# Every second normalization of the last block on VectorE, unread products moved ahead of the deviation, and two block orders replaced, in a four-part residual kernel on one Trainium2 core

## The chip, the cores and the metric

The kernel runs on one core of one Trainium2 chip. The metric is the device time of one execution in microseconds (us). It was taken in three timed runs; one more execution was profiled. The engines are TensorE (PE; its weight loads are shown as PEld), VectorE (DVE), ScalarE (ACT), GpSimd (POOL) and SyncE (SP), which issues most of the transfers. Each engine takes its own instructions in the order in which they were recorded, and they wait for each other by semaphores.

## The reference

x is 128 sequences of 64 tokens with 256 features, in float32. Four parts are added to it in turn, each conditioned on one vector per sequence:

```python
x = x + L0(x, cond)   # kx = modulated_linear(x); softmax attention over 16 heads of one token; modulated_linear
x = x + L1(x, cond)   # up(relu(down(x))) + x, with weights scaled by sequence
x = x + L2(x, ...)    # below
x = x + L3(x, cond)   # a matrix per sequence of rank 30, and a bias
```

The change lies in L2, which normalizes each token three times:

```python
def _ln(x, g, b):
    m = jnp.mean(x, axis=-1, keepdims=True)
    v = jnp.mean((x - m) ** 2, axis=-1, keepdims=True)
    return (x - m) * jax.lax.rsqrt(v + EPS) * g + b
h = _ln(x, pw_g[pathway_ids], pw_b[pathway_ids])      # gains gathered by token
h = _ln(h, cp_g[compartment_ids], cp_b[compartment_ids])
t = _ln(x, tm_g[time_steps], tm_b[time_steps])        # s is alike, with ms_g, ms_b
cat = concatenate([w[0]*h, w[1]*t, w[2]*m, w[3]*n, w[4]*r, w[5]*s])
return _ln(silu(cat @ int_W1 + b1) @ int_W2 + b2, int_g, int_be)
```

Here t and s share the deviation of x, so there are three sets of statistics: of x, of the gathered state h, and of the second layer's output y.

## The kernel before, in words

The 8192 tokens are worked on in 16 blocks (0 to 15) of 512 tokens (8 sequences), each of 4 tiles of 128 tokens. A prologue makes what doesn't depend on the tokens. For each block `attention` does L0 and `rest` does L1, L2 and L3. Block n + 1's attention is worked on beside block n's rest; after block 15's attention nothing is left to run beside its rest but what remains of block 14.

The program first lists all operations with their reads and writes, and a planner (`Plan`) then puts them in an order. Within an engine it picks among the operations that can start first the one of the lowest priority number. The numbers come from tables written into the kernel (`TURNS`): one for the prologue, one each for the first, second, last but one (14) and last (15) block, and one for the middle blocks; a block's number times 400 is added. The planner also hands out buffers, among them four PSUM banks for everything but the attention scores. What the planner emits is the order of each engine's queue.

The steps of `rest` that matter, with the lines of the profile before:

- The two up-products of L1 (L1223) give, with VectorE (L1236), the state x2T, which is features by tokens. TensorE transposes it (L1273), ScalarE copies the four tiles out (L1276), and VectorE makes the statistics (L469, L470).
- `rstd` and `offset` run on GpSimd: add epsilon (L474), the mean negated (L1253), the power -1/2 (L476), and the product of the two (L1254). They leave r and nr for x, rh and nrh for h, and ry and nry for y.
- `normalize` (L1259) is an ACTIVATE of ScalarE with scale r and bias nr, one for each tile.
- GpSimd multiplies and adds the gathered gains (L1284, L1290), whose gathers it issues itself (L940). h is normalized, xn and h are transposed (L1308), ScalarE copies them out (L1311), gains are products with a one-hot matrix (L1317) that VectorE multiplies in (L1326).
- The first layer's products (L1344 with weights w_x, w_t, w_s, w_h, and L1353 for biases), tanh (ScalarE, L1359) and VectorE (L1362) give s2. The second layer's products (L1387, one pair for each tile), an eviction with a bias (VectorE, L1392) and statistics follow.
- y is normalized (L1259 again) and scaled by GpSimd (L1403), which also adds x2 (L1406). TensorE transposes (L1418). In the last block alone the transposes take the normalized tiles themselves, VectorE evicts them with gain and state (L1424), and GpSimd's two steps run beside that. L3's two products (L1445, L1471) with VectorE between (L1456) follow, VectorE adds the tile (L1479), and SP writes it out (L1483).

In the last block (`quick`) six groups of unread products stand between the second layer and L1418. A group (`keep`) is one small product that reads its gate, and so waits for it (L444), and then n products of the identity with itself (L446) into a bank that nobody reads. Gates and n before: mvy, ry and nry with 4 each, and the first three normalized tiles with 3 each.

The wider attention steps that the order moves are the scores (L1071), their maxima (VectorE, L1080), the shift (L1121), the exponentials (ScalarE, L1135), the products with the values (L1146), their transpose and reciprocal (VectorE, L1158, L1162), the scaling (GpSimd, L1165), a transpose (L1176) and the output projection (L982).

Of the kernel before, what the change touches and what calls it, by code (L numbers as in the profile page):

```python
# [13 lines left out]
ALU = mybir.AluOpType  # L14
# [8 lines left out]
NTILE = T // 128  # L23
# [35 lines left out]
class Plan:  # L59
# [163 lines left out]
    -10633 41137 464 10909 -44878 -11608 -42604 -45090 10155 -44468 -500 -500 -500 -500 -500 -500  # L223
# [53 lines left out]
    -945 -5006 28741 3292 -555 -2679 4333 19756 13246 29426 3507 42507 949 -1489 14772 22434 -2092 33522 31798 41815  # L277
    951 30003 36734 39833 31441 44287 36835 36712 48388 -2211 33995 35152 6414 18014 27987 -10794 26523 6071 13167
    215 -9627 40936 -4357 6419 10572 4571 -7266 41550 17576 2454 32076 31767 -2728 16615 41208 837 4340 8765 36154
    -10880 4665 -558 -2062 4662 -3798 1273 31044 36706 35521 -1668 -419 19391 3818 26245 31507 24910 28317 -6286  # L280
    26998 -11618 25996 12900 26677 40415 20947 4197 4591 -10897 34316 29621 46596 6494 -4361 -5325 30488 28382 33266
    18048 33066 30258 -4468 44044 39446 3045 11442 54 3568 3791 -5774 -2389 836 17585 32107 3610 3509 11677 27998
    5918 -289 -3076 10611 22471 8317 24462 31609 27367 -11407 5640 5006 25531 6317 12721 12013 -6353 39363 7446 4072
    -1182 -2303 33420 5842 -3197 -3385 30659 31515 868 756 5023 33464 5290 34805 27086 29256 -2628 -4019 6625 33507
    3780 1799 30520 32280 29029 46575 20997 32367 9369 29333 -3611 1761 5073 23038 -2673 4124 -3837 18828 -210 5311
    32964 13572 -5042 815 27152 -6571 45385 6618 32189 18218 25530 13431 4354 28866 27343 42996 27711 28905 48852
    20499 25821 12505 19373 -5371 3342 27949 30404 6752 33874 -4408 26737 -9042 5014 33335 43087 44864 12794 42849
    4268 28770 21167 7601 9132 29149 5277 5277 5277 29004 31538 -2220 3845 8107 955 30135 3881 -4854 -7113 4074 30336
    11443 -2251 -580 -6078 4549 -2314 4266 11515 36765 1109 1500 5145 34519 17201 5779 33709 -5975 31030 14097 11178
    37473 23054 11112 -11491 27939 12681 11926 21735 35542 -1369 28928 27461 806 30077 -4774 23069  # L290
    """,
    "last": """
    -918 -4932 28785 3332 -569 37576 95 19583 13303 29612 3564 42657 5172 -1432 14778 22470 -2127 33487 31798 41753
    970 30025 36750 39866 31463 44309 36857 36734 48399 29838 33987 35461 6445 18036 28009 -10772 26548 6113 13077
    237 -9611 40952 -4341 6378 10566 11434 -7289 41527 17553 -2664 32185 32004 -2665 16815 41408 1037 4540 8965 36354
    -10831 4624 -604 -2085 4601 -3493 1256 17026 36681 35506 -1449 -434 19376 3801 25885 18811 24911 28352 -6303
    26981 -11699 25941 12883 26660 40398 20930 37525 4574 -10945 34299 29411 46591 6473 3726 -5383 30451 28410 33294
    18120 33105 30216 -4508 44002 39404 2964 11361 -166 3348 3579 -5994 -2333 610 18563 31899 3363 3325 4560 27779
    5744 -463 -3063 10622 -5376 8328 24473 31758 33518 -11396 5316 4677 43337 5936 12777 11684 -6037 39679 7352 3989
    -1170 -2067 33534 5696 -3081 -3304 30916 3513 1082 969 -1348 33586 5412 34403 27208 29378 -11701 -4005 6612 27354  # L300
    3767 1811 -9041 32275 33374 46570 20992 32362 9366 29381 -3588 1701 5121 4398 17015 4312 -3658 31671 -173 5447
    33077 13685 12794 -1508 27373 -6586 45375 6606 32445 18219 25520 13404 4325 28839 16940 42969 36247 29019 48820
    20465 25794 12337 -1583 -5541 3161 27768 30224 6612 33693 -4589 26551 -9304 4752 33073 42825 44576 12454 42500
    3902 28515 20894 7574 8848 28753 4872 4872 4993 28720 31263 -2335 3579 7833 -1601 29984 3730 -5005 -7186 4016
    30266 11356 -2321 -666 -6056 7806 -2377 11778 11029 36263 589 994 4678 34088 16701 5288 33069 -6488 30973 13881
    11108 37403 22984 11042 -11060 27869 3313 11805 21661 19322 -1441 28856 27558 772 29993 -4858 10564
# [5 lines left out]
def resid_chain(ctx: ExitStack, tc: tile.TileContext, a: dict, out: bass.AP, nblk: int = NBLK):  # L312
# [8 lines left out]
    nc = tc.nc  # L321
# [869 lines left out]
    def rest(blk, x1T, pw, oh, wdn, wup, tab, uT):  # L1191
# [64 lines left out]
        def normalize(dst, src, r, nr, tl):  # L1256
            act(
                256,
                lambda: nc.scalar.activation(  # L1259
                    dst.t, src.t, AF.Identity, bias=nr.t[:, tl : tl + 1], scale=r.t[:, tl : tl + 1]  # L1260
                ),
                [src, r, nr],
                [dst],
                more=0.186,
            )
# [130 lines left out]
        if quick:  # L1396
            for value in (mvy, ry, nry):
                keep(4, (value, lambda value=value: value.t.rearrange("p n k -> p (n k)")[:, :4] if value is mvy else value.t))
        for tl in range(NTILE):
            normalize(yn[tl], x3[tl], ry, nry, tl)  # L1400
            if quick and tl < NTILE - 1:
                keep(3, (yn[tl], lambda tl=tl: yn[tl].t[:, :4]))
# [206 lines left out]
```

## Time and profile before

| | us |
|---|---|
| timed runs | 897.63, 900.80, 904.46 |
| median | 900.8 |
| profiled execution | 894.98 |
| its span | 893.2 |

Shares of the span: TensorE 93%, VectorE 71%, GpSimd 68%, weight loads 60%, ScalarE 50%. In the slices of the page the granted clock of TensorE is full between the prologue and the last slices. The chain that ended last is TensorE's for 54% of the span, GpSimd's for 18%, VectorE's for 13%, ScalarE's for 6% and transfers' for 3%.

How to read the lines of the timeline: start and busy time in us, engine, line of the kernel, operation, output and input by the program's names, shapes, and how many; in brackets the time for which the engine stood idle before, and what ended it. A wait for several semaphores is put down to the one that came last. The profiled execution is a single one; its row durations are used as they are.

### The profile page before, as it was taken

The page shows a single profiled execution, that of the slowest core. Times are in us where ns is not written, and L with a number is a line of the kernel's source. Part 1 is how long each engine was busy: PE and PEld are TensorE (multiplying, and loading weights), DVE is VectorE, ACT ScalarE, POOL GpSimd, SP SyncE. Part 2 cuts the span into 40 slices and gives each one's busy share as a digit, 9 for nine tenths or more (in the row PEclk, how much of TensorE's full clock was granted, in tenths as well). Part 3 has the DMA queues.
Part 4 walks back from the last instruction along what each step waited for, and adds up shares of the span by engine and source line. Part 5 has one row for each costly group of instructions (what it writes and reads, how often), then busy time and mean ns, then how long its engine had stood idle before and what let it go on. Part 6 is the DMA issues. An engine that isn't in the chain of part 4 may idle for free.

```text
span 893.2 us, 24076 instructions
## 1 busy us (share of the span) xinstructions
PE 830.2 (93%) x9806; PEld 539.8 (60%) x9806; DVE 638.4 (71%) x1365; ACT 446.9 (50%) x825; POOL 608.0 (68%) x826
## 2 busy tenths in 40 slices
PE   4669999999999999999999999999999999999886
PEld 3548746656665756666566657566666667565435
DVE  3779867868685878777785858777776858586533
ACT  1454444545564555545555645555555556453330
POOL 5563673949687695959596886959595968845333
PEclk9889999999999999999999999999999999999998
DMA  8768742233423242332334232423324332102000
GB/s 252 210 160 251 243 127 64 67 85 103 123 84 116 73 119 82 95 94 73 117 88 125 85 111 69 128 77 92 101 74 117 84 97 84 48 11 64 1 24 25
DMA packets 62575, 90.24 MB, mean 101 GB/s; under 512 B 6328, under 2 KB 46200, under 8 KB 62464
## 3 DMA queue, kind: packets, MB, share of 16 engines
q1 hardware_dynamic: 57344, 71.92, 28.1%
q0 software_dynamic: 5120, 16.78, 6.0%
q8 instruction: 77, 1.26, 0.6%
q14 instruction: 34, 0.28, 0.1%
HBM read 75.44 MB, written 13.24 MB: 99 GB/s over the span
## 4 chain that ended last, share of the span: by engine, by line
PE 54%; POOL 18%; DVE 13%; ACT 6%; issue 5%; DMA 3%; SPq 0%; DVEq 0%; ACTq 0%; POOLq 0%
PE bank L1344 19%; PE sc L1071 4%; PE bank L982 4%; PE bank L1387 4%; PE bank L1015 4%; PE bank L1146 4%; DVE mt L1080 3%; POOL wdn L956 2%; PE sc L1121 2%; POOL kxe L1029 2%; PE bank L1058 2%; PE bank L1176 2%; POOL uu L1290 2%; PE bank L1317 1%; POOL xsT L925 1%
## 5 line engine op out<-in xcount | busy, mean ns | idle before, releaser
L1135 ACT ACTIVATE e<-sc 128x1024 f32<-128x1024 f32 x128 | 125.9, 1023 | 78.3 <-PE sc L1121 78.3
L1080 DVE TENSOR_REDUCE mt<-sc 128x8 f32<-128x1024 f32 x128 | 151.9, 1205 | 16.2 <-PE sc L1071 13.6
L1165 POOL TENSOR_TENSOR att<-ao,rz 128x256 f32<-128x256 f32 x45 | 28.1, 625 | 76.2 <-DVE rz L1162 75.9
L1326 DVE TENSOR_TENSOR uu<-uu,bank 128x512 f32<-128x512 f32 x96 | 63.9, 681 | 16.4 <-PE bank L1317 15.8
L1015 PE MATMUL bank<-wk,xsT 128*128 128x256 f32 x256 | 71.0, 413 | 0.9 <-POOL xsT L925 0.8
L1344 PE MATMUL bank<-uu,w_s 128*128 128x512 f32 x128 | 66.7, 604 | 0.8 <-DVE uu L1326 0.8
L1344 PE MATMUL bank<-uu,w_t 128*128 128x512 f32 x128 | 65.0, 618 | 0.5 <-DVE uu L1326 0.5
L1344 PE MATMUL bank<-x2T,w_x 128*128 128x512 f32 x128 | 64.7, 607 | 0.0
L1387 PE MATMUL bank<-w,uu 128*128 128x256 f32 x256 | 61.8, 385 | 1.9 <-DVE uu L1362 1.9
L1015 PEld LDWEIGHTS bank<-wk,xsT 128*128 128x128 f32 x256 | 48.8, 202 | 19.1 <-issue 11.1
L982 PE MATMUL bank<-osT,wo 128*128 128x512 f32 x128 | 59.2, 604 | 0.5 <-DVE osT L1181 0.5
L1344 PE MATMUL bank<-uu,w_h 128*128 128x512 f32 x128 | 58.7, 595 | 0.5 <-DVE uu L1326 0.4
L474 POOL TENSOR_SCALAR ry<-mvy 128x4 f32<-128x4 f32 (+1 forms) x19 | 4.4, 232 | 77.7 <-DVE mvy L470 77.6
L1090 ACT COPY mt<-mt 128x16 f32<-128x16 f32 x64 | 13.1, 204 | 84.4 <-DVE mt L1080 84.4
L469 DVE BATCH_NORM_STATS2 st<-uu 128x6 f32<-128x256 f32 x119 | 48.5, 418 | 8.1 <-ACT uu L1276 5.0
L1029 POOL TENSOR_TENSOR kxe<-kxe,kbr 128x256 f32<-128x256 f32 x64 | 46.8, 732 | 9.0 <-DVE kxe L1023 6.6
L1387 PEld LDWEIGHTS bank<-w,uu 128*128 128x128 f32 x256 | 45.9, 190 | 9.4 <-DVE uu L1362 3.1
L1023 DVE TENSOR_TENSOR kxe<-bank,dmk 128x256 f32<-128x256 f32 x64 | 26.8, 419 | 30.3 <-PE bank L1015 25.6
L956 POOL TENSOR_TENSOR wdn<-gdb,late 128x512 f32<-128x512 f32 x32 | 40.6, 1272 | 11.4 <-PE bank L1205 6.0
L940 POOL DMA_INDIRECT pw<-in_pw,idx x39 | 40.0, 1024 | 8.0 <-issue 7.4
L970 POOL TENSOR_TENSOR wup<-wup,ubb 128x512 f32<-128x512 f32 x32 | 40.6, 1269 | 3.7 <-DMA ubb<-ugub 1.5
L1103 ACT ACTIVATE mX<-bank,early 128x128 bf16<-128x128 f32 x64 | 23.6, 369 | 38.3 <-PE bank L1096 38.3
(217 smaller groups left out, 2135.9 us busy)
## 6 DMA issues: line engine op xcount, KB each, us to landing
xT<-in_xT SPq DMA_DIRECT2D x32, 256.0 KB
gdb<-dgdb SPq DMA_DIRECT2D x16, 512.0 KB
ubb<-ugub SPq DMA_DIRECT2D x32, 256.0 KB
wup<-ugub SPq DMA_DIRECT2D x32, 256.0 KB
dmk<-demod_k SPq DMA_DIRECT2D x30, 256.0 KB
out_x<-uu SPq DMA_DIRECT2D x35, 128.0 KB
ud<-uu SPq DMA_DIRECT2D x8, 512.0 KB
uT<-ud SPq DMA_DIRECT2D x16, 256.0 KB
```

The costliest lines, as they stand in the source:

```text
L469: dve(256, lambda: nc.vector.bn_stats(st.t, x.t), [x], [st])
L940: lambda tl=tl, n=n: nc.gpsimd.indirect_dma_start(out=pw[tl].t, out_offset=None, in_=a["pw"], in_offset=bass.IndirectOffsetOnAxis(ap=idx[: ...
L956: lambda w=w, dp=dp: nc.gpsimd.tensor_tensor(w(), gdb.t[:, :, 0:64], dp, ALU.mult),
L970: pool(1.25, lambda w=w: nc.gpsimd.tensor_tensor(w(wup), w(wup), w(ubb), ALU.add), [wup, ubb], [wup])
L982: nc.tensor.matmul(ps.t, owT[:, c, bass.ts(oc, 128)], osT.t[:, c, :], start=(c == 0), stop=(c == C - 1))
L1015: nc.tensor.matmul(ps.t[:, :F], xsT.t[:, c, bass.ts(tl, 128)], kwT[:, c, :], start=(c == 0), stop=(c == C - 1))
L1029: lambda: nc.gpsimd.tensor_tensor(kxe.t[:, :, 0:D], kxe.t[:, :, 0:D], heads(kinds["kbr"][0]), ALU.add),
L1080: lambda two=two: nc.vector.tensor_reduce(mt.t[:, two, 0:4], sc.t[:, two, :].rearrange("p q (g n) -> p q g n", g=4), AX.X, ALU.max),
L1135: lambda k=k: nc.scalar.activation(es[k].t, sc.t[:, 2 * k : 2 * k + 2, :], AF.Exp, scale=0.25),
L1326: lambda ps=ps, src=src, dst=dst, c=c: nc.vector.tensor_tensor(dst.t[:, c, :], src.t[:, c, :], ps.t, ALU.mult),
L1344: lambda ps=ps, w=w, src=src, fc=fc, c=c, n=n: nc.tensor.matmul(ps.t, w.t[:, c, bass.ts(fc, 128)], src.t[:, c, :], start=(n == 0 and c == ...
L1387: nc.tensor.matmul(ps.t[:, :F], s2.t[:, c, bass.ts(tl, 128)], w2.t[:, c, :], start=(c == 0), stop=(c == C - 1))
```

## The change

`normalize` takes every second tile (1 and 3) of the last block to VectorE, as a TENSOR_SCALAR with two columns (multiply, add), for all three normalizations of the block. Six instructions leave ScalarE's queue and stand in VectorE's. The groups of unread products get new gates and sizes: the four evicted tiles of the second layer with 3 each, mvy with 2, ry with 2; nry and the normalized tiles are no longer gates. That is 6 gates and 16 unread products in place of 6 and 21. Their six priorities go from -500 to 9000. Both tables of 14 and 15 are replaced as a whole.

```diff
--- before.py
+++ after.py
     "prologue": """
...
-    -10633 41137 464 10909 -44878 -11608 -42604 -45090 10155 -44468 -500 -500 -500 -500 -500 -500
+    -10633 41137 464 10909 -44878 -11608 -42604 -45090 10155 -44468 9000 9000 9000 9000 9000 9000
...
     "last but one": """
-    -945 -5006 28741 3292 -555 -2679 4333 19756 13246 29426 3507 42507 949 -1489 14772 22434 -2092 33522 31798 41815
...
+    25677 -9159 -4970 30441 -3888 33267 7456 2098 33469 22707 27320 30575 2712 35226 25625 29202 4770 2224 6807 48124
...
     "last": """
-    -918 -4932 28785 3332 -569 37576 95 19583 13303 29612 3564 42657 5172 -1432 14778 22470 -2127 33487 31798 41753
...
+    1830 -11952 33325 34973 32324 30258 13163 7005 30022 29679 4280 13204 14222 32365 21347 34327 15721 34598 36025
...
         def normalize(dst, src, r, nr, tl):
+            if quick and tl % 2:
+                dve(
+                    256,
+                    lambda: nc.vector.tensor_scalar(
+                        dst.t, src.t, r.t[:, tl : tl + 1], nr.t[:, tl : tl + 1], ALU.mult, ALU.add
+                    ),
+                    [src, r, nr],
+                    [dst],
+                    0.05,
+                    pair=True,
+                )
+                return
             act(
                 256,
...
         if quick:
-            for value in (mvy, ry, nry):
-                keep(4, (value, lambda value=value: value.t.rearrange("p n k -> p (n k)")[:, :4] if value is mvy else value.t))
+            for tl in range(NTILE):
+                keep(3, (x3[tl], lambda tl=tl: x3[tl].t[:, :4]))
+            keep(2, (mvy, lambda: mvy.t.rearrange("p n k -> p (n k)")[:, :4]))
+            keep(2, (ry, lambda: ry.t))
         for tl in range(NTILE):
             normalize(yn[tl], x3[tl], ry, nry, tl)
-            if quick and tl < NTILE - 1:
-                keep(3, (yn[tl], lambda tl=tl: yn[tl].t[:, :4]))
```

Lines from L1257 on stand 12 lower in the changed kernel (L1418 is L1430, L1479 is L1491, and so on), and L1260 is VectorE's normalization.

What the new tables do to the queues, as the two built programs show it:

- All queues are the same up to TensorE's up-products of block 13 (L1223); what follows differs on every engine. TensorE's and ScalarE's products and copies are the same ones, in another order.
- Block 13 to 14: the shift L1121 stands behind the transposes L1273 instead of ahead of them; on VectorE the transpose L1158 stands between the two maxima; on ScalarE two key copies stand ahead of the third normalization; on GpSimd the scaling L1165 stands behind five h operations instead of three.
- Block 15's attention: its last scores and value products stand two to four first-layer products earlier; between the last value products and the last attention transpose stand two short products (L1353), and all four second-layer products of block 14 follow the transpose.
- Block 15's rest: six of the eight transposes L1273 stand ahead of block 14's L1418; ScalarE's two copies of block 14's state stand ahead of the fourth tile's copy; half of block 14's last products (L1471) stand between the products with w_t.
- The end: the first group of unread products stands between the second and the third second-layer product, the other groups behind the fourth, and the transposes L1418 behind the group of ry. VectorE's last four additions start with tile 0, which is the last that GpSimd finishes.

## The prediction

> **What bounds the kernel now.** I read the page first (its busy shares, then the clock), then the chain of waits of the last 30 us, then the timeline of each engine there, then windows of one clock period. The page says that the kernel is limited by TensorE nearly everywhere:
>
> ```profile
> PE 830.2 (93%) x9806; PEld 539.8 (60%) x9806; DVE 638.4 (71%) x1365; ACT 446.9 (50%) x825; POOL 608.0 (68%) x826
> ```
>
> The two engine orders part for the first time at PE's up-products at 746.14 us, so only the last 147 us of the 893.2 can move. Until 834 PE there is nearly always busy; behind it the last block runs alone. Its end, as TensorE, GpSimd, ScalarE and VectorE did it (start, duration, line, count, and in brackets the idle time before):
>
> ```profile
> 871.34 3.72 PE L1387 MATMUL bank<-w,uu 128*128 128x256 f32 x16 [1.41 <-DVE uu L1362]
> 877.88 0.39 PE L444 MATMUL bank<-ry,ident 128*128 128x4 f32 x2 [1.70 <-POOL ry L476]
> 878.12 1.69 PE L446 MATMUL bank<-ident 128*128 128x128 f32 x8
> 879.60 0.43 PE L444 MATMUL bank<-nry,ident 128*128 128x4 f32 x2
> 879.89 2.05 PE L446 MATMUL bank<-ident 128*128 128x128 f32 x8
> ...
> 883.77 0.91 PE L446 MATMUL bank<-ident 128*128 128x128 f32 x6
> 884.52 0.27 PE L1418 MATMUL bank<-ident,uu 128*128 128x128 f32 x1
> ```
>
> ```profile
> 877.90 0.20 POOL L1254 TENSOR_TENSOR nry<-nry,ry 128x4 f32<-128x4 f32 x1
> 878.82 0.73 POOL L1403 TENSOR_TENSOR p<-uu,late 128x256 f32<-128x256 f32 x1 [0.71 <-ACT uu L1259]
> ...
> 883.72 0.72 POOL L1406 TENSOR_TENSOR uu<-uu,p 128x256 f32<-128x256 f32 x1
> ```
>
> ```profile
> 878.14 0.60 ACT L1259 ACTIVATE uu<-p,nry,ry 128x256 f32<-128x256 f32 x1 [7.58 <-POOL nry L1254]
> ...
> 879.63 0.58 ACT L1259 ACTIVATE uu<-p,nry,ry 128x256 f32<-128x256 f32 x1
> ```
>
> ```profile
> 888.40 1.16 DVE L1479 TENSOR_TENSOR p<-bank,p 128x256 f32<-128x256 f32 x3 [0.87 <-PE bank L1471]
> 889.48 0.42 DVE L1479 TENSOR_TENSOR uu<-bank,uu 128x256 f32<-128x256 f32 x1
> ```
>
> The reader is to see that the four normalizations are done at 880.21, but that the transposes, which need nothing else, start at 884.52: TensorE takes its queue in order, and the unread products stand in it until then. They are work on the path, not cover. The windows give the cause of half of it:
>
> ```profile
> 851.20:854.60 3.40, 2.12 (x13) 1.20 (x12) 2.81 (x8) 2.43 (x5) 3.40 (x6) 1.00 0.43 143
> 854.60:858.00 3.40, 3.40 (x5) 1.15 (x6) 1.35 (x5) 0.00 (x0) 2.47 (x6) 0.51 0.00 0
> 868.20:871.60 3.40, 1.99 (x6) 0.74 (x5) 1.38 (x2) 1.20 (x2) 0.00 (x0) 1.00 0.00 0
> 875.10:878.50 3.40, 1.70 (x14) 1.51 (x14) 1.06 (x5) 0.36 (x1) 1.66 (x4) 1.00 0.00 0
> 878.50:881.90 3.40, 3.40 (x19) 3.40 (x18) 0.00 (x0) 1.71 (x4) 3.08 (x5) 0.51 0.02 5
> ```
>
> Each row is a stretch: length, then busy time of PE, PEld, DVE, ACT, POOL, then the granted clock. Two thin stretches (1.70 and 2.12 us of PE in 3.4) are followed by one at clock 0.51; one with 1.99 is not (871.60 to 875 ran at 1.00), so the share alone doesn't decide.
>
> **The tail, from nry to the end.** Let R be the end of nry (878.10). Before: 893.20 - 878.10 = 15.10 us. In the new orders TensorE meets after R only the eight transposes; two normalizations are ScalarE's and two VectorE's.
> - TensorE's path: 0.04, two ScalarE normalizations (878.14 to 879.23, 1.09), 0.04, and from the transposes on the old 893.20 - 884.52 = 8.68: R + 9.85.
> - GpSimd's path: the eight multiplications and additions (878.82 to 884.44, 5.62) were hidden under unread products and now are not. They start behind VectorE's first normalization. No row of the last block shows it; the nearest is the prologue's 128x256 TENSOR_SCALAR by two columns (L747, mean 404 ns), against 590 of ScalarE. Then VectorE's four additions (888.40 to 889.90, 1.50; the first in the new order needs GpSimd's last result) and 3.30 to the end: R + 0.04 + 0.40 + 0.08 + 5.62 + 0.08 + 1.50 + 3.30 = R + 11.02.
> - VectorE's second normalization runs as GpSimd wants to start. In the prologue the same cast (L508, 128 wide rows, f32 to bf16) took 0.29 us at 47.57 and 1.15 at 43.48, beside a GpSimd operation that ended at 44.5; so one may hold the other. Bounds: 0 and the whole 0.40 (less the 0.08 that GpSimd waits anyway). I take 0.32: R + 11.34.
>
> So GpSimd takes TensorE's place as the last: 15.10 - 11.34 = **3.76 us less**. [...]
>
> **Unread products ahead of R.** The first x3 group of the new order stands between the second and the third second-layer product. One group of three with its gate took 0.12 + 0.77 = 0.89 in the chain (882.90 to 883.79, full clock). VectorE needs 0.86 a tile (872.50, 873.37, 874.23), as long as TensorE, so nothing hides it: **0.89 more**. The other groups run while statistics, ry and nry are made: from 875.96, three of 0.89 and two of 0.12 + 0.51 end at 879.9, and the transposes are wanted at R' + 1.17 = 880.16. That cover is thin: at clock 0.5 the groups would end at 883.9, TensorE's path would be 3.7 longer than R + 9.85, and would pass GpSimd's by 2.2.
>
> **Statistics of x and of the gathered state.** There VectorE takes two normalizations as well (1.09 instead of 2.07). Ahead of them the new order has ScalarE write both halves of block 15's transposed state (0.68 and 0.60) before the fourth tile's copy, which costs about 0.75 of that; and the first transposes (851.96) waited not for ScalarE but for a bank that VectorE's additions of 851.39 freed, which stays. Taken at nothing, between -0.7 and +0.7. VectorE's normalizations there stand before those additions, two to each wait for nr, at 0.8 us in a stretch where VectorE was idle (847.3 to 849.75). GpSimd's three gathers of the last block keep their place behind the h multiplications; SP's loads only swap neighbours, and no wait in this stretch ends on a DMA: nothing, or 1 us if a gather came late.
>
> **The orders.** TensorE's work is the same, so waits are counted, taking each engine's queue in its new order with the old rows:
> - Last but one block, 746 to 770: old waits 0.84 and 0.16. In the new order two key copies stand in ScalarE ahead of the third normalization, so the transposes of xn wait 0.5, the attention transposes 0.75 for GpSimd (its multiplication now stands behind five h operations instead of three) and a gain product 0.3; the sc shift moved behind the x2 transposes saves some. Net +0.65, bounds 0 and +1.4.
> - Last attention tiles, 808 to 835: old waits 0.49 + 0.83 + 0.52 = 1.84. New: after the last e-products only two short products cover the chain transpose, reciprocal, multiplication (832.43 to 834.20), so 1.25, but then four products cover the rest: about 1.4 in all. Net -0.4, bounds -1.2 and 0.
> - Last block, 854 to 870: the 0.78 wait before w_s (861.03) goes, since other products stand there, among them 0.35 of block 14's output. Net -0.43, bounds -2.2 (the half-clock stretch, 3.4 us for 1.7 of work, not entered) and +1.
>
> Sum: -3.76 + 0.89 + 0 + 0.65 - 0.40 - 0.43 = **-3.05 us**. The profiled execution took 894.98 (span 893.20); 891.93 is 0.9966 of it, and of the median 900.8 this is **897.7**. The profiled one lies below all three timed (897.63 to 904.46), so the ratio is used.
>
> [...]
>
> **Rivals.**
> - The orders close more than I can trace (0.30). The waits listed in PE's timeline from 800 to 871.34 add up to 8.9, and the half-clock stretch is 1.7. Two thirds of the first (5.9), the second, and the tail's 2.9 are 10.5: 890.2. For it: the waits come from short chains, which another order can cover. Against: the largest (1.31 for x1T, 1.41 for s2) stand in both orders behind the same instructions.
> - The cover fails (0.13): the clock halves in the unread products. The tail gains 0.66 instead of 2.87: about 900. For it: it halved at 878.50 in this trace. Against: the groups now leave no pause behind the products.
> - The new waits throttle TensorE through the last block (0.07), the side on which it is slower. Place: 844.5 to 870, where products of block 14 no longer fill the wait for x2T (843.2 to 844.5) and a wait of 0.7 for ScalarE's half appears. From 844.5 to 870 PE is busy for 23.3 us, 3.4 of them at half already; if three quarters of the other 19.9 ran at half they would cost 15, less the 3: 912. It decides from the point where most 3.4 us stretches are as thin as the two that were followed by a fall (1.70 and 2.12 us); the new waits alone do not make them so.
> - The change doesn't act: excluded for the normalizations (six instructions stand on VectorE instead of ScalarE), possible for the searched orders, which is in my range.
>
> **How the numbers follow.** The forecast has 0.50, its own range 893 to 901.5. Range over all: 888.5 to 902; it takes in the rival at 890.2 and leaves out the throttled one and outer tails. One per cent is 9 us, about what the three timed runs (6.8 apart) can tell. Faster by over 1%: the first rival, 0.30; slower: the throttled one with an outer tail, 0.08; within: 0.62.
>
> **What would show it.** Tail: transposes about 1.2 after nry, and VectorE's first L1491 waiting on GpSimd, not TensorE. Nry 0.9 later after the first second-layer product than 6.8 us. An unread group between second and third product. GpSimd's first multiplication 0.4 late. Wrong if the transposes still start behind unread products, if the last additions follow TensorE, or if the clock's low stretches multiply after 840.

## The result and the profile after

No measurable change. Fourteen runs of the changed kernel had a median of 901.89 us, fourteen of the kernel before beside them 903.02: ratio 0.9988, 95% interval 0.9968 to 1.0008. Run again later, beside runs of before with a median of 893.49, it was 1.0009 (0.9992 to 1.0027). The forecast was 0.9966.

The page of the changed kernel's profile begins:

```profile
span 900.1 us, 24059 instructions
...
PE 833.0 (93%) x9796; PEld 537.1 (60%) x9796; DVE 639.4 (71%) x1371; ACT 444.6 (49%) x819; POOL 608.0 (68%) x826
```

Its span is 6.9 us longer than before's, but it was 8.42 us behind where the programs part (754.56 against 746.14), so the spans can't be compared. The last stretch can: from the first up-product of block 13 to the end. Each kernel was profiled a second time (before_again, after_again, below). All stages are in us; "s2" is the end of VectorE's last L1374 (L1362 in before), "nry" the end of GpSimd's nry, called R in the prediction, and the stage from nry to the end of the span is the tail. Ends are taken from the span as the page rounds it, so the tail is good to 0.05.

| stage | before | before_again | after | after_again |
|---|---|---|---|---|
| block 13 to 14 (first up-products) | 49.22 | 49.21 | 52.02 | 51.03 |
| block 14 to 15 | 46.64 | 46.63 | 45.66 | 45.66 |
| block 15 to s2 | 29.28 | 27.60 | 28.28 | 28.28 |
| s2 to the end of nry | 6.82 | 6.81 | 7.28 | 7.29 |
| nry to the end of the span | 15.10 | 15.24 | 12.30 | 12.26 |
| last stretch | 147.06 | 145.49 | 145.54 | 144.52 |

The tail did become what the change set out to make of it. TensorE's timeline in the changed kernel (start, busy time; in brackets the wait before):

```profile
879.50 0.70 PE L1399 MATMUL bank<-w,uu 128*128 128x256 f32 x2 [0.33 <-DVE uu L1374]
880.57 1.56 PE L1399 MATMUL bank<-w,uu 128*128 128x256 f32 x6 [0.38 <-DVE uu L1374]
...
882.11 0.92 PE L446 MATMUL bank<-ident 128*128 128x128 f32 x6
882.86 1.89 PE L1399 MATMUL bank<-w,uu 128*128 128x256 f32 x8
...
888.08 0.69 PE L446 MATMUL bank<-ident 128*128 128x128 f32 x4
888.61 0.27 PE L1430 MATMUL bank<-ident,uu 128*128 128x128 f32 x1
```

GpSimd's and VectorE's timelines there:

```profile
887.60 0.20 POOL L1254 TENSOR_TENSOR nry<-nry,ry 128x4 f32<-128x4 f32 x1
888.40 0.77 POOL L1415 TENSOR_TENSOR p<-p,late 128x256 f32<-128x256 f32 x1 [0.60 <-DVE p L1260]
...
893.24 0.72 POOL L1418 TENSOR_TENSOR p<-p,p 128x256 f32<-128x256 f32 x1
```

```profile
887.84 0.42 DVE L1260 TENSOR_SCALAR p<-p,ry,nry 128x256 f32<-128x256 f32 x1 [1.94 <-POOL nry L1254]
888.17 0.41 DVE L1260 TENSOR_SCALAR uu<-uu,ry,nry 128x256 f32<-128x256 f32 x1
...
893.99 0.76 DVE L1491 TENSOR_TENSOR p<-bank,p 128x256 f32<-128x256 f32 x2 [2.16 <-POOL p L1418]
894.66 0.75 DVE L1491 TENSOR_TENSOR uu<-bank,uu 128x256 f32<-128x256 f32 x2
```

The transposes start 0.81 behind nry instead of 6.42, and VectorE's first addition waits 2.16 us for GpSimd. The last addition ends at R + 7.61, earlier than the forecast's R + 8.04. But from it to the end of the span are 4.69 us, where before has 3.30. The chain of waits of the profile ends at that addition and says nothing of this. The closing instructions of the queues do; before and after (queue, count, shortest/median/longest duration in ns, first and last start in us):

```profile
...
L1605 POOLq DRAIN  x3: 45/102/6078, 883.7 to 892.9; - x3
L1605 SPq DRAIN  x3: 7/7/7, 892.4 to 892.7; - x3
```

```profile
...
L1617 POOLq DRAIN  x3: 45/102/6635, 892.6 to 899.8; - x3
L1617 SPq DRAIN  x3: 7/7/7, 898.0 to 899.5; - x3
```

In both, GpSimd's queue ends with a DRAIN of more than 6 us (6.08 and 6.64). In before it lasted from 883.7 to 889.8, under TensorE's tail; SyncE, whose listed waits there have 0.8 us for the output transfers, came to its first drain at 892.4, later than the other engines to theirs, and to its last at 892.7. In the changed kernel it lasts from 892.6 to 899.2; SyncE is at its first drain at 898.0 and at its last only at 899.5. In both the DRAIN ends 5.3 us after GpSimd's last instruction (884.44 and 893.96).

### The profile page after: what moved, and what is told of

The parts are those of the page before. It is cut to its first block, busy times and chain, and to the rows that moved or that the text cites. A ratio compares the mean times of both kernels' runs of the same rounds, so it can differ in the third digit from the quotient of the medians.

```text
span 900.1 us, 24059 instructions
## 1 busy us (share of the span) xinstructions
PE 833.0 (93%) x9796; PEld 537.1 (60%) x9796; DVE 639.4 (71%) x1371; ACT 444.6 (49%) x819; POOL 608.0 (68%) x826
## 3 DMA queue, kind: packets, MB, share of 16 engines
q8 instruction: 77, 1.26, 0.6%
## 4 chain that ended last, share of the span: by engine, by line
PE 74%; DVE 10%; ACT 6%; issue 4%; POOL 3%; DMA 2%; SPq 0%; POOLq 0%; DVEq 0%; ACTq 0%
PE bank L1356 21%; PE sc L1071 8%; PE bank L1399 6%; PE bank L982 6%; PE bank L1146 6%; PE bank L1015 6%; DVE mt L1080 4%; PE bank L1058 2%; PE sc L1121 2%; PE bank L1176 2%; ACT uu L1323 2%; PE bank L1223 2%; PE bank L1329 2%; PE bank L1205 2%; PE bank L1430 1%
## 5 line engine op out<-in xcount | busy, mean ns | idle before, releaser
L1165 POOL TENSOR_TENSOR att<-ao,rz 128x256 f32<-128x256 f32 x45 | 28.0, 623 | 78.9 <-DVE rz L1162 70.0
L1338 DVE TENSOR_TENSOR uu<-uu,bank 128x512 f32<-128x512 f32 x96 | 63.6, 679 | 16.9 <-PE bank L1329 16.4
L1158 DVE STREAM_TRANSPOSE ao<-bank 128x512 f32<-128x512 f32 x45 | 32.0, 712 | 19.0 <-PE bank L1146 19.0
```

Of the source, the lines that this page charges most:

```text
L1338: lambda ps=ps, src=src, dst=dst, c=c: nc.vector.tensor_tensor(dst.t[:, c, :], src.t[:, c, :], ps.t, ALU.mult),
```

## The experiments

All twelve were made from the two kernels. The tables of orders can be exchanged, and the groups of unread products can be moved by their priority. Ratios are to before, in runs on the same chip.

**1. code_alone.** The new code with before's two order tables; the priority of the unread groups is raised so that all stand behind the fourth second-layer product.

```diff
-    -10633 41137 464 10909 -44878 -11608 -42604 -45090 10155 -44468 9000 9000 9000 9000 9000 9000
+    -10633 41137 464 10909 -44878 -11608 -42604 -45090 10155 -44468 60000 60000 60000 60000 60000 60000
...
     "last but one": """
-    25677 -9159 -4970 30441 -3888 33267 7456 2098 33469 22707 27320 30575 2712 35226 25625 29202 4770 2224 6807 48124
+    -945 -5006 28741 3292 -555 -2679 4333 19756 13246 29426 3507 42507 949 -1489 14772 22434 -2092 33522 31798 41815
...
     "last": """
-    1830 -11952 33325 34973 32324 30258 13163 7005 30022 29679 4280 13204 14222 32365 21347 34327 15721 34598 36025
+    -918 -4932 28785 3332 -569 37576 95 19583 13303 29612 3564 42657 5172 -1432 14778 22470 -2127 33487 31798 41753
...
```

> Both block orders are those of before; VectorE's normalizations and the new unread groups are in, and all six groups stand behind the fourth second-layer product. The 'last stretch' is measured from the first up-product of block 13 to the end of the span (before 147.06 us, after 145.54). Theory A (the tail gains what it gained in after, 2.80, and the order of the last-but-one block is what ate it): blocks 13 to 14 (first up-product to first up-product) take 49.3 as before, nry stays 6.8 behind the first second-layer product, the tail from nry to the end is 12.3, the half-clock stretch near the first products of block 15 is still there; last stretch 144.3, ratio to before 0.997. Rival B (the 4.69 us from the last addition to the end, against 3.30, were only that one execution's): tail 10.9, last stretch 142.9, ratio 0.995. Rival C (with before's orders the unread products run at half clock and TensorE ends last): tail 13.5 or more, ratio 0.999.

Ratio 1.0042 (1.0029 to 1.0056): slower, which none of the theories had. The tail is 12.29 as in A, and blocks 13 to 15 are before's, but block 15 to s2 takes 34.69 us. TensorE's waits from 841.5 to 876.3 (us in total, times, longest), the first three:

```profile
PE bank L1356 <- DVE uu L1338: 2.1, 2, 1.2
PE bank L1399 <- DVE uu L1374: 1.8, 1, 1.8
PE bank L1320 <- DVE uu L1260: 1.3, 1, 1.3
```

and VectorE's timeline where the third of them is made:

```profile
850.94 0.76 DVE L1491 TENSOR_TENSOR uu<-bank,uu 128x256 f32<-128x256 f32 x2 [0.96 <-PE bank L1483]
851.61 0.43 DVE L469 BATCH_NORM_STATS2 st<-p 128x6 f32<-128x256 f32 x1
...
852.86 0.38 DVE L1260 TENSOR_SCALAR uu<-uu,r,nr 128x256 f32<-128x256 f32 x1
```

The second of x's normalizations given to VectorE stands there behind block 14's last additions and two statistics of h, 4 us after nr was ready. The thin work is followed by stretches at half clock:

```profile
862.70:866.10 3.40, 1.99 (x5) 0.68 (x5) 1.88 (x3) 0.63 (x2) 0.00 (x0) 1.00 0.00 0
866.10:869.50 3.40, 3.40 (x5) 1.34 (x4) 0.00 (x0) 0.00 (x0) 0.00 (x0) 0.51 0.00 0
```

(length, busy PE, PEld, DVE, ACT, POOL, granted clock). There were three, from 856.0, 866.2 and 876.4.

**2. orders_alone.** Before's code with both new order tables.

```diff
     "last but one": """
-    -945 -5006 28741 3292 -555 -2679 4333 19756 13246 29426 3507 42507 949 -1489 14772 22434 -2092 33522 31798 41815
+    25677 -9159 -4970 30441 -3888 33267 7456 2098 33469 22707 27320 30575 2712 35226 25625 29202 4770 2224 6807 48124
...
     "last": """
-    -918 -4932 28785 3332 -569 37576 95 19583 13303 29612 3564 42657 5172 -1432 14778 22470 -2127 33487 31798 41753
+    1830 -11952 33325 34973 32324 30258 13163 7005 30022 29679 4280 13204 14222 32365 21347 34327 15721 34598 36025
...
```

> Both new orders, with all normalizations on ScalarE and the unread groups of before. Theory A (the new order of the last-but-one block costs about 2.7 us and the last block's order regains it): blocks 13 to 14 take 52.0 as in after, the first second-layer product comes 125 us after the first up-product of block 13 (before 125.20, after 124.94), then before's 6.8 and 15.1: last stretch 146.9, ratio to before 0.999 to 1.000. Rival B (the 52.0 was that execution's, as six of its middle blocks took 50.3 instead of 49.3 with the same instructions): blocks 13 to 14 between 49.3 and 50.3, last stretch 144.5, ratio 0.997.

Ratio 1.0014 (0.9997 to 1.0031), and the last stretch 145.49, the same as before_again's: theory A as to the ratio. Blocks 13 to 14 took 51.03 rather than 52.0, block 14 to 15 45.65, block 15 to s2 28.47, the tail 13.52: there was no half-clock stretch in its unread products, so TensorE reached the transposes at nry + 4.79 instead of 6.42. Rival B was half right: 1.0 of the 52.0 was that execution's, 1.8 are the order's.

**3. old_14_new_15.** The changed kernel with the last-but-one table of before; the unread groups are moved as in code_alone.

```diff
     "last but one": """
-    25677 -9159 -4970 30441 -3888 33267 7456 2098 33469 22707 27320 30575 2712 35226 25625 29202 4770 2224 6807 48124
+    -945 -5006 28741 3292 -555 -2679 4333 19756 13246 29426 3507 42507 949 -1489 14772 22434 -2092 33522 31798 41815
...
```

> The changed kernel with the last-but-one table of before, the new last table, and all unread groups behind the fourth second-layer product. Mixed tables make an order of their own behind the first scores product of block 14's second half; up to there it is before's. Theory A: blocks 13 to 14 at 49.3 to 50, and the last block as short as in after: last stretch 142 to 143, ratio to before 0.995, faster than the run with only the unread groups moved by 2 us. Rival B (the order of block 14 costs nothing): no faster than that run. Rival D (the two tables only fit together): blocks 13 to 14 at 52 or more again, or the gain lost by waits behind block 15's attention; last stretch 146 or more.

Ratio 1.0179 (1.0155 to 1.0203): rival D. Blocks 13 to 14 took 47.54, and block 15 to s2 34.27, but 14 to 15 took 60.45, with waits of 1.6 (L1176 for GpSimd), 1.3, 1.1, 1.0 and 0.8 us and half clock from 804.6 to 821.6. The two tables fit only together, so this run says nothing about the price of either.

**4. unread_behind.** The changed kernel with the first unread group moved behind the fourth product.

```diff
-    -10633 41137 464 10909 -44878 -11608 -42604 -45090 10155 -44468 9000 9000 9000 9000 9000 9000
+    -10633 41137 464 10909 -44878 -11608 -42604 -45090 10155 -44468 60000 60000 60000 60000 60000 60000
```

> The changed kernel, with the first unread group moved from between the second and third second-layer product to behind the fourth; nothing else differs. As forecast, the group costs 0.89 us there: from the end of the second half of s2 to the end of nry 6.4 us instead of 7.28, last stretch 144.6. Rival (VectorE's evictions and statistics set the pace, so that the group lay half hidden): 6.8 as in before, last stretch 145.1. Rival (the group keeps the clock, and without it the products behind run at half): 8 or more. Ratio to before 0.997 to 0.998, blocks 13 to 14 at 52.0 if the order makes them, 49.3 to 50.3 if that was the execution.

Ratio 0.9992 (0.9971 to 1.0013). From s2 to nry 6.38 instead of 7.28: the group costs 0.90, as forecast. The last stretch was 145.83 all the same, for TensorE ran at half clock from 841.7 to 848.5, in work that is instruction for instruction the changed kernel's, whose two profiles have no such stretch. Its windows, and those of after_again, where the same work comes 3.3 us later; both are laid whole clock periods from the falls of their own execution (last section):

```profile
838.30:841.70 3.40, 1.66 (x33) 1.09 (x32) 1.61 (x3) 2.46 (x5) 2.69 (x5) 1.00 0.00 0
841.70:845.10 3.40, 1.98 (x64) 1.80 (x64) 1.28 (x2) 0.00 (x1) 2.95 (x5) 0.50 0.00 0
845.10:848.50 3.40, 3.37 (x16) 3.27 (x16) 1.50 (x6) 1.89 (x5) 0.00 (x0) 0.50 0.02 5
```

```profile
842.79:846.20 3.41, 2.17 (x92) 1.92 (x92) 0.70 (x1) 1.41 (x4) 3.41 (x6) 1.00 0.00 0
846.20:849.61 3.41, 2.00 (x20) 1.73 (x16) 2.39 (x7) 1.51 (x5) 1.77 (x3) 1.00 0.00 0
```

**5. yn_only.** Before's orders and code up to the fourth second-layer product; only y's tiles 1 and 3 go to VectorE, with the new unread groups behind. The tables and the priority are exchanged as in code_alone; the rest of the edit, against the changed kernel:

```diff
-        def normalize(dst, src, r, nr, tl):
-            if quick and tl % 2:
+        def normalize(dst, src, r, nr, tl, other=False):
+            if other and quick and tl % 2:
...
-            normalize(yn[tl], x3[tl], ry, nry, tl)
+            normalize(yn[tl], x3[tl], ry, nry, tl, True)
```

> Before's orders and before's instructions up to the fourth second-layer product; only y's normalizations of tiles 1 and 3 go to VectorE, and the unread groups are the new ones, all behind the fourth product. Theory E (in code_alone it was VectorE's normalizations of x and h, queued behind statistics in an order not made for them, that cost 5 us in the last block): the first second-layer product comes 125.2 us after the first up-product of block 13 as in before (130.6 in code_alone), nry 6.4 to 6.8 behind it, the tail 12.3; last stretch 144.1, ratio to before 0.997. Rival F (the new unread groups and the tail are what throttles, wherever the normalizations of x and h are): ratio 1.003 as in code_alone. Rival G (clock stretches fall on another place in every execution, and code_alone's 5 us were those): first second-layer product anywhere from 123 to 130, ratio as E.

Ratio 0.9970 (0.9954 to 0.9986): theory E. The last stretch is 142.60, the tail 12.34, s2 to nry 6.81. The first second-layer product came 123.5 us behind block 13's first up-product instead of 125.2, because no half-clock stretch fell on the products with w_t here.

**6. two_tiles_dve.** The changed kernel, with the gain product and the addition of x2 of tiles 0 and 2 on VectorE.

```diff
+            if quick and tl in (0, 2):
+                dve(256, lambda tl=tl: nc.vector.tensor_tensor(x3[tl].t, yn[tl].t, lg, ALU.mult), [yn[tl]], [x3[tl]])
+                dve(
+                    256,
+                    lambda tl=tl: nc.vector.tensor_tensor(x3[tl].t, x3[tl].t, x2[tl].t, ALU.add),
+                    [x3[tl], x2[tl]],
+                    [x3[tl]],
+                )
+                continue
             pool(0.65, lambda tl=tl: nc.gpsimd.tensor_tensor(x3[tl].t, yn[tl].t, lg, ALU.mult), [yn[tl]], [x3[tl]])
```

> The changed kernel, with the gain product and the addition of x2 of tiles 0 and 2 of the last block on VectorE instead of GpSimd: GpSimd has four of these instructions left instead of eight and should end 2.75 us earlier, at nry + 3.45 instead of 6.16. In all profiles with VectorE's normalizations the span ends 6.1 us after GpSimd's last instruction, and in the trace GpSimd's queue has a DRAIN there of 6.6 us; in before GpSimd ends early and the span ends 3.3 us after VectorE's last addition. Theory H (GpSimd's closing drain sets the end): the drain ends about nry + 8.7, the additions go by VectorE's path (four more instructions of 0.42 ahead of the evictions), at nry + 6.0 to 7.5, and the end is 3.3 behind them: tail 10.8 instead of 12.3, ratio to before 0.997. Rival I (the output transfers are slower when four additions come close together): 4.7 behind the additions again, tail 12.2, ratio 0.999.

Ratio 0.9984 (0.9971 to 0.9997). The span ends 3.36 us after the last addition, not 4.7: theory H, rival I falls. The tail is 11.74 and not 10.8: both engines slowed each other, and TensorE's last products ran at half clock (1.24 us instead of 0.71). VectorE's and GpSimd's timelines:

```profile
876.75 0.96 DVE L1416 TENSOR_TENSOR p<-uu,late 128x256 f32<-128x256 f32 x1
877.63 0.94 DVE L1416 TENSOR_TENSOR uu<-p,late 128x256 f32<-128x256 f32 x1
...
880.68 0.41 DVE L1419 TENSOR_TENSOR uu<-uu 128x256 f32<-128x256 f32 x1
```

```profile
877.38 0.91 POOL L1424 TENSOR_TENSOR uu<-uu,late 128x256 f32<-128x256 f32 x1
```

Together 0.96 and 0.91 us, alone 0.41 (880.68) and 0.72.

**7. back_transposed.** As yn_only, without GpSimd's eight instructions: the state is turned back by TensorE into the bank of the last product.

```diff
+                    for c in range(C if quick else 0):
+                        nc.tensor.matmul(pso[i].t[:, bass.ts(c, 128)], x3T.t[:, c, bass.ts(2 * two + i, 128)], ident, start=(c == 0), stop=False)
...
-                    nc.tensor.matmul(pso[i].t[:, :F], zT.t[r, :], vw[r, :], start=True, stop=True)
+                    nc.tensor.matmul(pso[i].t[:, :F], zT.t[r, :], vw[r, :], start=not quick, stop=True)
```

> As yn_only, but in the last block GpSimd's eight instructions behind nry are gone: TensorE turns the state back (two products with the identity for each tile, into the bank of its last product), so that the sum stands in PSUM, and VectorE and ScalarE copy two tiles each. GpSimd's last instruction is then nry itself, and its drain ends at about nry + 5.3. Theory H: the end follows TensorE's path: transposes at nry + 1.7, from there the 8.68 us of before, 0.7 less for copies on two engines and 0.4 more for the products: tail 10.1, last stretch 141.9 to 142.3 with before's clock stretches, ratio to before 0.994 to 0.996. Rival I (slow transfers after close additions): tail 11.5. Rival J (the products with the identity run at half clock in the thin tail): 1 us more.

Ratio 0.9966 (0.9949 to 0.9983), last stretch 141.9. The end is 3.31 behind the last copy, so the drain is hidden (H); the tail is 11.62 instead of 10.1, because each pair of tiles takes TensorE 1.09 us to turn back, twice, mostly on the path.

**8. before_again.** Before, unchanged, for a second profile.

> Before once more, for a second profile. If TensorE's half-clock stretches belong to the program, they stand again 38.6 and 14.8 us ahead of the end, and the last stretch is 147.1 within 0.5. If their place is the execution's, they stand elsewhere or are absent, at distances that are multiples of 3.41 us from each other, and the last stretch differs by 1.7 us for each.

The last stretch was 145.49. The half-clock stretch at the products with w_t, which the prediction took for the program's, was not there; the one in the unread products was. The windows of one clock period where the first had stood, and around the second:

```profile
850.20:853.60 3.40, 2.41 (x15) 1.29 (x14) 2.25 (x7) 2.98 (x6) 3.40 (x7) 1.00 0.47 155
853.60:857.00 3.40, 3.11 (x9) 1.46 (x9) 2.60 (x7) 0.00 (x0) 2.55 (x6) 1.00 0.00 1
872.80:876.20 3.40, 1.70 (x15) 1.51 (x15) 1.22 (x5) 0.20 (x1) 1.66 (x4) 1.00 0.00 0
876.20:879.60 3.40, 3.40 (x18) 3.40 (x18) 0.00 (x0) 1.87 (x4) 2.92 (x5) 0.51 0.02 5
```

**9. after_yn_only.** The changed kernel's orders, x and h normalized by ScalarE; unread groups behind the fourth product. The edit against the changed kernel is that shown for yn_only, and the priority 60000.

> The changed kernel's orders, but x and h are normalized by ScalarE as in before; y's tiles 1 and 3 stay on VectorE, and all unread groups stand behind the fourth second-layer product. It differs from yn_only in the orders alone, and from unread_behind in who normalizes x and h. Theory K (the orders cost 1.8 us in block 14 and give 1.0 back in block 15's attention, and on VectorE x and h gain nothing): 1 us slower than yn_only, ratio to before 0.998, the tail 12.3. Rival L (with the new orders VectorE's x and h are what shortens the last block): first second-layer product 1 us later than in unread_behind behind the first product with w_t, ratio 0.9995 or more.

Ratio 1.0021 (1.0005 to 1.0037). It differs from yn_only (0.9970) in the orders alone: they cost more than theory K's 1 us. Its profile shows 146.99 against 142.60, of which two half-clock stretches (from 845.3 and 872.6) are a part. L can't be told: the stretch at 845.3 lies in the part compared (block 15 to s2 29.57, against 28.28 in after_again and 28.47 in orders_alone, which had none).

**10. split_gain.** Before's orders. GpSimd multiplies by the gain before the deviation is known; behind nry it has nothing left, and VectorE, ScalarE and TensorE do the rest. With g the gain, y*g = (x3*g)*r + g*nr.

```diff
+            pool(0.65, lambda tl=tl: nc.gpsimd.tensor_tensor(x3g[tl].t, x3[tl].t, lg, ALU.mult), [x3[tl]], [x3g[tl]])
...
+                    lambda tl=tl: nc.vector.scalar_tensor_tensor(xt[tl].t, lg, nry.t[:, tl : tl + 1], x2[tl].t, ALU.mult, ALU.add),
...
+                lambda tl=tl: nc.vector.scalar_tensor_tensor(x3g[tl].t, x3g[tl].t, ry.t[:, tl : tl + 1], xt[tl].t, ALU.mult, ALU.add),
...
+                    nc.tensor.matmul(held[i].t[:, :F], ident, x2[i].t, start=True, stop=False)
```

> Before's orders up to the fourth second-layer product. GpSimd multiplies the evicted tiles by the gain before the deviation is known (four instructions ahead of ry), ScalarE and VectorE add the rest behind it (VectorE four scalar_tensor_tensor with r, and for tiles 2 and 3 the mean's part and x2; for tiles 0 and 1 TensorE puts x2 into the bank of the last product ahead of time in place of the unread groups of mvy and ry). GpSimd has nothing behind nry, and TensorE meets its transposes 0.6 us earlier than in yn_only. Theory H (GpSimd's drain set the end in yn_only): the end goes by TensorE's path of the forecast, transposes at nry + 1.15 and 8.68 behind it, tail 9.9 to 10.4; nry up to 0.3 later since GpSimd is busy ahead of ry; ratio to before 0.994 to 0.995, faster than all others. Rival M (VectorE's eight extra instructions are the new last): tail 11.5, ratio 0.996.

Ratio 0.9945 (0.9923 to 0.9966), the lowest of all (the interval overlaps those of yn_only and back_transposed), last stretch 140.1: theory H. GpSimd is done with nry, and TensorE's transposes follow 1.10 behind it:

```profile
874.88 0.20 POOL L1254 TENSOR_TENSOR nry<-nry,ry 128x4 f32<-128x4 f32 x1
```

```profile
876.18 0.27 PE L1460 MATMUL bank<-ident,uu 128*128 128x128 f32 x1
```

The span ends at nry + 9.72; the forecast had TensorE's path at R + 9.85. GpSimd's DRAIN (5.56 us from 874.8) is over at 880.4, long before the end at 884.8.

**11. yn_and_x.** As yn_only, with x's tiles 1 and 3 on VectorE too.

```diff
-            normalize(xn[tl], x2[tl], r, nr, tl)
+            normalize(xn[tl], x2[tl], r, nr, tl, True)
```

> As yn_only, and x's tiles 1 and 3 on VectorE too (h stays on ScalarE), in before's orders. In code_alone's trace VectorE's second normalization of x stood behind block 14's additions and two statistics, and the transposes of xn waited 1.26 us for it; h's stood at 0.73 for two without a wait. Theory E1 (x is the culprit): the first product with w_t 1.2 us later than in yn_only, and with thinner work ahead of it more half-clock stretches; ratio to before 1.001 to 1.004. Rival E2 (h is): as yn_only, 0.997.

Ratio 1.0007 (0.9989 to 1.0024), 0.37 percentage points above yn_only: x is part of the loss (E1), and E2, by which it would have been h alone, falls. Block 15 to s2 took 30.98 against 27.59, with one half-clock stretch (from 856.4), and the transposes of xn waited for VectorE, as in code_alone:

```profile
853.85 0.77 PE L1320 MATMUL bank<-ident,uu 128*128 128x128 f32 x5 [1.26 <-DVE uu L1260]
```

The first product with w_t waited another 1.24 us, for VectorE's L1338, and came 2.4 us later than in yn_only, twice what E1 had. The rest of code_alone's loss comes with h; h without x was not tried.

**12. after_again.** The changed kernel once more.

> The changed kernel once more, on the chip of the other experiments and with a second profile. In the first profile its identical middle blocks took 50.3 us in six cases instead of 49.3. If blocks 13 to 14 take 51.0 here as in the three other runs with this order, 1.0 of the 52.0 was that execution's. GpSimd's last instruction at nry + 6.2 and the end at nry + 12.3 as in all runs with eight GpSimd instructions behind VectorE's normalization; from the end of s2 to nry 7.28. Last stretch 144.5 plus 1.7 for each half-clock stretch; ratio to before 0.998 to 1.000.

As expected: blocks 13 to 14 at 51.03, s2 to nry 7.29, GpSimd's end at nry + 6.15, the span's at nry + 12.26; last stretch 144.52 without a half-clock stretch ahead of the tail's end.

## Why the prediction was wrong

Against before's second profile, term by term:

| step | forecast | measured |
|---|---|---|
| the orders, up to s2 | -0.18 | +1.53 |
| first unread group, s2 to nry | +0.89 | +0.48 |
| the tail | -3.76 | -2.98 |
| sum | -3.05 | -0.97 (0.11%) |

Two steps failed, and the baseline of the tail held a stretch at half clock that is not in every execution.

**"...+ 1.50 + 3.30".** The 3.30 us from VectorE's last addition to the end was carried over as if it followed that addition. It did so in before only because GpSimd had been done 8.8 us before the end. With GpSimd made the last engine, its closing DRAIN became the last thing: GpSimd's end at R + 6.16, 5.3 us of DRAIN and 0.8 of closing, so R + 12.3 in all eight profiles that have GpSimd's eight instructions behind VectorE's normalization (12.24 to 12.34). The term measured 4.69 for 3.30. The order of the engines in the tail was right, and GpSimd's end came 0.3 us earlier than summed (R + 6.46): its first instruction, beside VectorE's second, took 0.05 longer than usual (0.77), not 0.32. The 0.32 rested on a cast of the prologue, which is 96x256 in the trace and not 128 wide, and was the whole VectorE instruction; the two overlapped for 0.18 us only (888.40 to 888.58). In all, the step cost 1.0 us of the forecast (12.30 for 11.34). Three experiments show it: with GpSimd's work shortened (two_tiles_dve), gone (back_transposed) or moved ahead (split_gain), the end is 3.3 to 3.4 behind VectorE's last instruction again.

**The orders: "TensorE's work is the same, so waits are counted", with "+0.65", "-0.40", "-0.43".** Measured +1.82 (block 13 to 14), -0.97 and +0.68. The orders alone do this: orders_alone has the same 51.03 and 45.65. The counting of waits was not what failed in sum: from the first up-product of block 13 to s2, length less busy time of PE is 123.49 - 112.41 = 11.08 in before_again and 124.97 - 113.92 = 11.05 in after_again. What failed is that the same work takes the same time. Block 13 to 14 in before_again and after_again:

```profile
745.71:794.92 49.21, 48.06 (x598) 31.08 (x597) 36.70 (x81) 26.90 (x49) 37.27 (x51) 1.00 0.17 50
748.38:799.41 51.03, 49.49 (x597) 31.19 (x596) 36.33 (x80) 26.93 (x49) 36.59 (x50) 1.00 0.17 49
```

TensorE's idle time grows by 0.39 there (1.15 to 1.54; the forecast had 0.65), its busy time by 1.43. The two numbers of products differ by one record. Over all three stages the busy time is 1.5 us longer for the same instructions; 0.7 of that is the first second-layer product, which now lies ahead of s2's end. Why the other 0.8 is longer stays open; busy times rest on modelled ends.

The waits only changed place. TensorE's longest from the first up-product of block 13 to s2 (us in total, times, longest), before and after:

```profile
PE bank L1399 <- DVE uu L1374: 1.9, 2, 1.4
PE sc L1121 <- DVE mTb L1110: 1.7, 2, 0.8
...
PE bank L1176 <- POOL att L1165: 0.8, 1, 0.8
...
PE bank L1285 <- DVE x2T L1236: 0.4, 1, 0.4
```

```profile
PE bank L1176 <- POOL att L1165: 2.4, 4, 1.4
PE bank L1285 <- DVE x2T L1236: 1.4, 1, 1.4
...
PE sc L1121 <- DVE mTb L1110: 0.8, 1, 0.8
...
PE bank L1399 <- DVE uu L1374: 0.3, 1, 0.3
```

What the shift L1121 (-0.9) and s2 (-1.6) no longer wait, the attention transposes wait for GpSimd (+1.6) and block 15's transposes for its state (+1.0). The third rival named this last wait (for x2T, no longer filled by block 14's products), but the sum had no term for it. My argument that the 1.41 for s2 "stand in both orders" was wrong: the new order starts the first second-layer product on the first half of s2.

**The baseline of the tail: "Before: 893.20 - 878.10 = 15.10 us".** The profiled execution had two stretches at half clock ahead of its end, and I took both for the program's. The one in the unread products stands in the 15.10. It is in both profiles of before, but not in orders_alone, which runs the same instructions there: 13.52 from nry to the end. So the tail's gain is 2.98 against an execution with the stretch and 1.26 against one without. How often before has it, three profiles don't tell; the timed gain of yn_only, 2.7 us with an interval of 1.3 to 4.1, doesn't settle it. The other stretch, at the products with w_t (1.7 us), the sum left out; it stood in a bound and in the first rival. It is absent from the second profile, and it is nearly all of the 1.52 us by which the last stretch is shorter in after than in the first profile of before. The falls lie on a grid of 3.413 us whose phase is the execution's: 1.3 us from the span's start in before, 2.4 to 2.5 in before_again (last section).

**What held.** The unread group costs 0.90 (unread_behind), as summed; the net is 0.48 because the first product's early start gives part of it back. VectorE's x and h at nothing: 28.28 against 28.47 in orders_alone. In before's order, however, they cost about 6 us (code_alone against yn_only, 1.0042 against 0.9970 of 893), so that part of the code is bearable only with the new orders, and with them what y's normalization gains is lost again (1.0009 for the whole change). The forecast weighed the code only under the new orders; y's part alone, with the old orders, gives 0.9970, nearly the forecast's 0.9966.

**The rivals.** The orders did not close waits (first rival). The unread products ran at full clock in every profile with the new groups, so the cover did not fail (second). A last block lengthened by waits and half-clock stretches (third) is what code_alone and old_14_new_15 show; the changed kernel doesn't.

Why after_yn_only and yn_only differ by 0.5%, more than the 1.5 us of the orders, is open: half-clock stretches are part of it in the profiles, but one profile of each doesn't tell how often they come. The timed runs also set after_yn_only (1.0021) above unread_behind (0.9992), which differs only in that VectorE takes half of x and h; the intervals overlap a little, so that these normalizations gain something under the new orders is possible and not shown.

## What to carry to other kernels

Before taking an engine off the end of a kernel, look at the closing instructions of each queue: here GpSimd, once it was the last engine, brought a DRAIN that ended 5.3 us after its last instruction, and the chain of waits, which ends with the last arithmetic instruction, doesn't show it. Work of GpSimd behind the last dependence was worth moving ahead of it, as (x3*g)*r + g*nr does, even though others then do more (split_gain, 0.9945). Take two profiles of a baseline before crediting a change with a half-clock stretch, and measure an edit of code under the old order first: a searched order can hide what the code costs or gains.

## What the runs showed of the hardware

- **The clock's grid.** Falls of TensorE's clock in one execution lie whole multiples of 3.413 us apart: in before 154.9, 854.6, 878.5, 888.8 (205, 212 and 215 periods from the first), in code_alone 856.0, 866.2, 876.4 (3 and 6), in after_yn_only 845.3, 872.6, 886.2 (8 and 12), in yn_and_x 856.4 and 887.1 (9). The grid's phase differs from execution to execution (counted from the span's start it is 1.3 us in before, 2.4 to 2.5 in before_again, 3.1 in after_again), and with it how the same work is cut into periods: in unread_behind a period with 1.66 us of TensorE's work was followed by half clock, while in after_again the same work fell into periods with 2.17 and 2.00 and was not. In six profiles (before and after from 130 us on, after_again, after_yn_only, yn_and_x and split_gain over about their last 145 us) every period of the grid at full clock with less than 1.6 us of modelled work was followed by half clock (0.8 to 1.5 us) and none with more than 2.5; in between both occur (half clock behind 2.48 and 2.12 in before, none behind 1.7 in yn_and_x and split_gain).
- **GpSimd's closing DRAIN** ended 5.3 us after its last instruction, whether that was nry itself (split_gain: 880.4 behind 875.1) or came at nry + 6.2 (after: 899.2 behind 893.96).
- **VectorE beside GpSimd.** In two_tiles_dve VectorE's 128x256 f32 products took 0.94 to 0.96 us beside GpSimd's, its last addition of that size, alone, 0.41; GpSimd's took 0.91 instead of 0.72. The TENSOR_SCALAR of the change cost GpSimd only 0.05 us (0.77 against 0.72) in 0.18 us of overlap.
- **One program, two block times.** In the first execution of the changed kernel six of the identical middle blocks took 50.3 to 50.5 us and the others 49.4; in before and in four of the experiments' profiles nearly all took 49.2 to 49.3. TensorE's listed waits of such a long block were only 0.4 to 0.6 us more (1.6 against 1.0 to 1.2); the rest is open.
